# Spreading 128 node numbers over the partitions: two small DMAs through DRAM in place of a scaled identity and a product with ones

## The chip, the cores and the metric

The kernel runs on one core of a Trainium2 chip. Its metric is the device time of one execution in microseconds (us). Five engines work side by side, each through its own instructions in order, and they meet through semaphores: TensorE (PE: matmuls, with its weight loads shown apart as PEld), VectorE (DVE), ScalarE (ACT), GpSimd (POOL) and SyncE (SP), which here only issues DMAs. POOL issues DMAs too: the scatters that add rows of a tile to rows of a table in DRAM.

## What is computed

One layer of a graph network over 6,250 nodes with 128 features and 200,000 edges, sorted by `dst`:

```python
h = jnp.maximum(_layernorm(x, axis=-1), 0.0)
xw = h @ W_in                                            # a table of nodes
W_ij = shifted_softplus(f_ij @ W_f1 + b_f1) @ W_f2 + b_f2   # for each edge
W_ij = W_ij * f_ij_cutoff
x_ij = xw[dst] * W_ij
out = segment_sum(x_ij, src, num_segments=6250)
x = x + shifted_softplus(out @ W_o1 + b_o1) @ W_o2 + b_o2
```

`dst` is sorted, so the gather reads narrow windows of the table. `src` is random, so the sum over edges is the hard part.

## The kernel before

Edges are worked on in 391 groups of 512, called quads. A software pipeline written out by hand runs one iteration `i` for each quad and a few more at the end. In iteration `i` PE multiplies the gathered rows and the filter of quad `i-1` (L336, L339, L347), starts the filter of quad `i+1` (L289) and finishes quad `i-2`. ACT takes the soft plus of quad `i` (L294, L295, L300), DVE the product of quad `i-1` (L357). Further work hangs on named points of an iteration ("L", "D0", "D1", "A0", "DM", "PE2", "A2", "D2", "S", in that order of the text) through `at(iteration, point, function)`. The text's order is the order on each engine.

There are two kinds of quads.

- **Plain quads** (239). For each chunk of 128 edges PE multiplies an equality matrix with the messages, so that edges with the same node are summed in the chunk (L369). ACT copies the result to the tile `s` (L377, five buffers), DVE and ACT make the row numbers (L391, L398), and POOL issues four scatters that add the rows to an accumulator in DRAM (L417). That makes 955 scatters.
- **Permuted quads** (152: 8, 10, 13, 15, 18, 20 and so on, two and three apart in turn). A permutation on PE (L527) sorts the edges into 16 groups of nodes with 32 places each. Eight such quads are then summed at once by "units" (L605, L620, L631) into an accumulator in SBUF. Edges for which a group has no place left go to 64 overflow rows (L542 to L544), and ACT copies those to a tile `mo` (L550).

The overflow rows of two permuted quads make one tile of 128 rows, and a short chain takes each such pair to one more scatter (76 in all). For a pair whose second quad is `q`:

- `over_idx` (L558, DVE, iteration `q+5`): the node number of each row, a column `so` (shown as `ovs`) with one number for each partition.
- `over_dg` (L563 and L566, ACT, `q+6`): the 128x128 identity scaled by that column, and a small term `ojd` for the row number of the scatter.
- `over_row` (L571, PE, `q+6`): a matrix of ones times the scaled identity. Now each partition holds all 128 node numbers, in PSUM.
- `over_eq` (L576, DVE, `q+7`, point D0, the first of that iteration on DVE): which rows have the same node.
- `over_sum` (L581, PE, `q+8`), `over_copy` (L586, ACT), `over_ji` (L591, DVE), `over_int` (L595, ACT) and `over_scatter` (L417, POOL), all in `q+9`: rows of the same node are summed, and POOL scatters the sums.

Because quads lie two and three apart, `q` is a multiple of 5, and the pattern of hooks repeats every five iterations. `q+6` is even for one pair and odd for the next. `clear` moves a hook past iterations that hold a unit (they are multiples of 5 too).

SP issues, in every even iteration, the loads of two quads, `load_sc`: the features `ft` (L270), the node numbers `sb` (L272), the places `rb` (L275, two), four window numbers that are read into registers (L277), and four windows of the table `wn` (L282). Each waits for its buffer to come free. SP also issues the table's and features' loads and stores (L151, L233, L239, L259 to L261, L654). All of this is one queue in order.

PSUM has four banks with the tag "B" for the products `pp`, `pq`, `po`, `orow`, `osum` and `un`. The list `banked` names functions that take such a bank at the point PE2. An iteration with more than two of them is `full`, and then ACT copies `pp` within the same iteration, not early in the next.

The scatters go to four accumulators in turn (`acc_of`: three of them in the first 140 and in the last 64). A scatter waits for the landing of the one before it on the same accumulator. `scat` counts scatters by iteration, to place the early reading of accumulator 0. After the last scatter a tail reads the accumulators, sums them and applies the output layers (L1075 to L1138).

Of the kernel before, what the change touches and what calls it, by code (L numbers as in the profile page):

```python
# [7 lines left out]
F32 = mybir.dt.float32  # L8
# [5 lines left out]
ALU = mybir.AluOpType  # L14
# [6 lines left out]
P = 128  # L21
# [25 lines left out]
def tile_gnn(ctx: ExitStack, tc: tile.TileContext, x, fB, cT, srcT, srcr, dstr, win_, wf1, wf2, bias, bo1c, wo1,  # L47
             wo2, consts, ident, out, n_edges):
    nc = tc.nc
# [24 lines left out]
    mpi = {q: n for n, q in enumerate(mpq)}  # L74
    units = unit_its(mpq)
    plain = {q: n for n, q in enumerate(q for q in range(NQ) if q not in mpi)}
    scat = [0] * (NQ + 12)
# [1 line left out]
        if q not in mpi:  # L79
            scat[q + 4] += min(4, NCH - 4 * q)  # L80
    for q in mpq[1::2] + mpq[-1:] * (len(mpq) % 2):
        scat[q + 10] += 1
    RET = max(120, sum(scat) - 64)
    ret_at = min(i for i in range(len(scat)) if sum(scat[:i + 1]) >= RET)

    cp = ctx.enter_context(tc.tile_pool(name="cp", bufs=1))
    dp = ctx.enter_context(tc.tile_pool(name="dp", bufs=1, space=DRAM))
    edge = ctx.enter_context(ExitStack())
    ld = edge.enter_context(tc.tile_pool(name="ld", bufs=3))
    wk = edge.enter_context(tc.tile_pool(name="wk", bufs=2))  # L90
    sp_ = edge.enter_context(tc.tile_pool(name="sp", bufs=5))
    ps = edge.enter_context(tc.tile_pool(name="ps", bufs=2, space=PSUM))

    accs = []
    for k in range(NACC):
        a_ = dp.tile([ACC_R, P], F32, name=f"acc{k}")
        accs.append(a_)
    tab = dp.tile([NP * 3, P], BF16, name="tab")
    reld = dp.tile([NSC, SC], BF16, name="reld")
    src16 = dp.tile([NSC, SC], I16, name="src16")  # L100
# [7 lines left out]
    idt = cp.tile([P, P], F32, name="idt")  # L108
# [14 lines left out]
    iot = iotw[:, GN // 2:]  # L123
    tri = cp.tile([P, P], BF16, name="tri")
    onesb = cp.tile([P, P], BF16, name="onesb")
    onesf = cp.tile([P, P], F32, name="onesf")
    thr = cp.tile([P, GRP - 1], F32, name="thr")
    ge = cp.tile([P, 4 * RKQ, GRP + 1], BF16, name="ge")
    dropT = cp.tile([P, EP // P], BF16, name="dropT")
# [291 lines left out]
    mp = {}  # L421
# [136 lines left out]
        nc.vector.scalar_tensor_tensor(so, mo[:, P + 2:P + 3], float(GN), mo[:, P + 1:P + 2], op0=ALU.mult, op1=ALU.add)  # L558
        mp[q]["so"] = so

    def over_dg(q):
        dg = wk.tile([P, P], F32, tag="dg", name="dg", bufs=1)
        nc.scalar.mul(dg, idt, mp[q]["so"])  # L563
        mp[q]["dg"] = dg
        jd = sp_.tile([P, 2], F32, tag="ojd", name="ojd", bufs=3)
        nc.scalar.activation(jd[:, 0:1], mp[q]["so"], AF.Identity, bias=off)  # L566
        mp[q]["jd"] = jd

    def over_row(q):
        t = ps.tile([P, 512], F32, tag="B", name="orow", bufs=4)  # L570
        nc.tensor.matmul(t[:, :P], onesf, mp[q]["dg"], start=True, stop=True)  # L571
        mp[q]["row"] = t

    def over_eq(q):
        eq = wk.tile([P, P], F32, tag="oeq", name="oeq", bufs=1)
        nc.vector.tensor_scalar(eq, mp[q].pop("row")[:, :P], mp[q]["so"], None, op0=ALU.is_equal)  # L576
        mp[q]["eq"] = eq

    def over_sum(q):
# [90 lines left out]
    with tc.manual_schedule():  # L670
# [26 lines left out]
        onesc = cp.tile([P, 1], F32, name="onesc")  # L697
        nc.vector.memset(onesc, 1.0)
        nc.vector.memset(onesb, 1.0)
        nc.vector.memset(onesf, 1.0)  # L700
        nc.vector.memset(dropT, 0.0)
        nc.vector.memset(ge[:, :, 0:1], 1.0)
        nc.vector.memset(ge[:, :, GRP:], 0.0)
# [74 lines left out]
        def at(i, point, fn, *a):  # L778
            hooks.setdefault((i, point), []).append((fn, a))
# [121 lines left out]
        for r in range(-(-len(mpq) // RKQ)):  # L901
            i = mpq[RKQ * r]
            at(i - 5, "D2", rank_group, r)
            k = clear(i - 4, units)
            at(k, "PE2", rank_count, r)
            at(k + 1, "D0", rank_own, r)
            k = clear(k + 1, units)
            at(k, "PE2", rank_over, r)
            at(k + 1, "D0", rank_slot, r)
        for q in mpq:  # L910
            at(q + 1, "D2", perm_oh, q)
            at(q + 2, "D2", part_rem, q, 1)
            at(q + 2, "D2", part_rem, q, 2)
            for s in range(4):
                at(q + 3 + s // 2, "PE2", permute, q, s)
                at(q + 4 + s // 2, "A0", perm_out, q, s)
            at(q + 4, "PE2", over_pe, q)
            at(q + 5, "A0", over_out, q)
            if q == mpq[-1] and mpi[q] % 2 == 0:
                at(q + 4, "D2", over_none, q)  # L920
            if mpi[q] % 2 or q == mpq[-1]:
                at(q + 5, "DM", over_idx, q)
                at(q + 6, "A0", over_dg, q)
                k = clear(q + 6, units)
                at(k, "PE2", over_row, q)
                at(k + 1, "D0", over_eq, q)
                k = clear(q + 8, units)
                at(k, "PE2", over_sum, q)
                at(k + 1, "A0", over_copy, q)
                at(k + 1, "DM", over_ji, q)  # L930
                at(k + 1, "A2", over_int, q)
                at(k + 1, "S", over_scatter, q)
        last = mpq[-1]
        for r in range(len(mpq) // RND):
            for s, k in enumerate(unit_slots(mpq, r)):
                at(k - 1, "D2", unit_oh, r, s)
                at(k, "PE2", unit_pe, r, s)
                at(k + 1, "D1", unit_evac, r, s)

        banked = (prep_tp, prep_mm, rank_count, rank_over, permute, over_pe, over_row, over_sum, late_bias, r0_tp)  # L940
        full = {-1: False}
        r0_end = r0_at
        s1_pe(0)
# [63 lines left out]
    with tc.For_i(0, trips, 1) as ci:  # L1007
# [43 lines left out]
        eq = wk.tile([P, P], F32, tag="eq", name="feq")  # L1051
# [129 lines left out]
def unit_its(qs):  # L1181
    return {i for r in range(len(qs) // RND) for i in unit_slots(qs, r)}


def clear(i, busy, n=1):
    while any(i + k in busy for k in range(n)):
        i += 1
    return i
# [114 lines left out]
```

## Time and profile before

| | before |
|---|---|
| median of 3 runs | 2117.85 us (2117.82 to 2121.36) |
| the profiled execution | 2119.3 us |
| its span, first to last instruction | 2117.0 us |
| mean granted TensorE clock | 0.971 |
| PE / ACT / DVE / POOL busy, share of the span | 90% / 85% / 83% / 80% |
| scatters | 955 and 76, from 49.2 us to 2060.1 us |
| SP's longest wait | 510.3 us in 132 times, for DVE's L318 |

How to read the views. A row of the groups of instructions gives line, engine, operation, out<-in, shapes and count, then the busy time in us and the mean ns of one, then the time that the engine was idle just before them and what ended it. A row of the timeline gives start and length in us, engine, line, operation and count, with the idle time before it and what ended it in brackets. A row of the stretches gives each engine's busy time and number of instructions between two times. "issue" is idle time in which the engine waited for nothing that the profile shows.

### The profile page before, as it was taken

Reading aid. Unit: us, or ns where it says so; the run is one execution under the profiler, and the core shown is the slowest. Engines: PE = TensorE matmul, PEld = TensorE weight load, DVE = VectorE, ACT = ScalarE, POOL = GpSimd, SP = SyncE. Lnnn points to the kernel's source line nnn. Section 1 sums busy time; section 2 is a strip of 40 time slices with the busy share of each in tenths; the row PEclk is TensorE's granted clock in tenths of the full one; section 3 lists DMA queues with packets and bytes.
Section 4 is the critical chain, followed back from the end, with each engine's and each line's share of the span. In section 5 each row is a group of like instructions: output and inputs, shape, how many; then the busy total and the mean of one; then the engine's idle time right before and its main releaser. Section 6 shows DMA issues by size and latency. Waiting matters only on the chain.

```text
span 2117.0 us, 56533 instructions
## 1 busy us (share of the span) xinstructions
PE 1915.6 (90%) x19769; PEld 1392.3 (66%) x19769; DVE 1763.7 (83%) x4710; ACT 1789.3 (85%) x4781; POOL 1695.6 (80%) x1073
## 2 busy tenths in 40 slices
PE   3778999999999999998989999999999999998946
PEld 2556667676666667666767677777767666766724
DVE  4768888888989898888898989889888878897825
ACT  4688889998988899898989999999899898988804
POOL 2678888888888888888888888888888888887874
PEclk9899999999999999999999999999999999999977
DMA  7987767777777777777777777777777777777639
GB/s 265 242 183 132 149 129 146 141 157 144 149 141 147 133 151 145 141 145 142 148 133 157 139 136 152 143 146 152 136 146 139 129 152 137 139 154 144 111 38 241
DMA packets 395696, 315.17 MB, mean 149 GB/s; under 512 B 94959, under 2 KB 335130, under 8 KB 395410
## 3 DMA queue, kind: packets, MB, share of 16 engines
q1 hardware_dynamic: 245858, 240.57, 38.9%
q0 software_dynamic: 149264, 70.91, 35.3%
q8 instruction: 155, 2.54, 0.5%
q14 instruction: 131, 1.07, 0.2%
q10 hardware_dynamic: 288, 0.07, 0.0%
HBM read 173.32 MB, written 138.06 MB: 147 GB/s over the span
## 4 chain that ended last, share of the span: by engine, by line
PE 32%; ACT 20%; DVE 19%; DMA 10%; POOL 10%; issue 7%; SPq 2%; ACTq 0%; DVEq 0%; POOLq 0%
POOL acc L417 10%; DMA acc<-s,ji 8%; PE un L620 8%; PE W L347 7%; PE pq L527 6%; ACT xc L352 5%; PE pp L369 4%; ACT mst L533 3%; DVE so L605 3%; ACT e L295 3%; ACT e L294 2%; ACT e L300 2%; DVE pm L503 2%; ACT s L377 2%; DVE a L324 1%
## 5 line engine op out<-in xcount | busy, mean ns | idle before, releaser
L417 POOL DMA_INDIRECT acc<-s,ji x955 | 1538.3, 1611 | 350.3 <-issue 222.8
L527 PE MATMUL pq<-pt,pm 128*128 128x387 bf16 x2432 | 484.1, 339 | 26.5 <-ACT s L377 19.2
L352 ACT ACTIVATE xc<-xg,cb 128x128 f32<-128x128 f32 x1564 | 446.4, 374 | 46.9 <-PE xg L339 45.0
L347 PE MATMUL W<-w,a 128*128 128x128 f32 x3128 | 461.7, 292 | 0.0
L347 PEld LDWEIGHTS W<-w,a 128*128 128x128 f32 x3128 | 386.2, 194 | 41.8 <-issue 2.3
L620 PE MATMUL un<-so,mst 32*128 32x392 bf16 x7296 | 355.1, 331 | 41.8 <-DVE pr L467 18.4
L527 PEld LDWEIGHTS <-pm 128*128 128x128 bf16 x2432 | 238.6, 99 | 187.7 <-issue 36.1
L620 PEld LDWEIGHTS <-mst 32*128 32x128 bf16 x7296 | 223.0, 94 | 169.3 <-issue 63.0
L324 DVE SCALAR_TENSOR_TENSOR a<-z,e 128x512 f32<-128x512 f32 x391 | 267.2, 683 | 70.2 <-ACT e L300 70.0
L300 ACT ACTIVATE e<-e,con 128x512 f32<-128x512 f32 x391 | 282.3, 722 | 12.7
L369 PEld LDWEIGHTS pp<-m,eq 128*128 128x128 f32 x1912 | 255.0, 195 | 37.2 <-DVE accT L631 23.6
L369 PE MATMUL pp<-m,eq 128*128 128x129 f32 x1912 | 261.4, 280 | 17.0 <-DVE accT L631 15.0
L533 ACT CAST mst<-pq 128x387 bf16<-128x387 f32 x608 | 260.4, 480 | 8.3 <-PE pq L527 8.3
L377 ACT COPY s<-pp 128x258 f32<-128x258 f32 x478 | 167.1, 391 | 116.2 <-PE pp L369 64.8
L295 ACT ACTIVATE e<-e 128x512 f32<-128x512 f32 x391 | 246.5, 630 | 12.4
L294 ACT ACTIVATE e<-z 128x512 f32<-128x512 f32 x391 | 242.0, 619 | 16.7 <-PE z L289 16.1
L357 DVE TENSOR_TENSOR m<-W,xc 128x512 f32<-128x512 f32 x239 | 164.0, 686 | 80.4 <-ACT xc L352 75.4
L517 DVE TENSOR_TENSOR pt<-pt 128x512 f32<-128x512 f32 x304 | 209.9, 691 | 0.0
L503 DVE TENSOR_SCALAR pm<-iot,pos 128x576 bf16<-128x576 f16 x608 | 197.5, 387 | 0.0
L631 DVE TENSOR_TENSOR accT<-un,accT 128x392 f32<-128x392 f32 x288 | 142.5, 556 | 47.3 <-PE un L620 32.1
L357 DVE TENSOR_TENSOR pt<-W,xc 128x512 f32<-128x512 f32 x152 | 104.5, 688 | 82.1 <-ACT xc L352 80.7
L289 PE MATMUL z<-ft,ws 123*128 123x512 bf16 x391 | 151.9, 389 | 17.9 <-DMA ft<-fsd 17.9
(156 smaller groups left out, 2693.2 us busy)
## 6 DMA issues: line engine op xcount, KB each, us to landing
sb<-src SPq DMA_DIRECT2D x195, 256.0 KB
ft<-fsd SPq DMA_DIRECT2D x195, 240.0 KB
rb<-reld SPq DMA_DIRECT2D x391, 64.0 KB
fsd<-f SPq DMA_DIRECT2D x49, 480.0 KB
fb<-in_fB_dram SPq DMA_DIRECT2D x49, 320.0 KB
fsd<-f SPq DMA_DIRECT2D x49, 320.0 KB
acc<-s,ji POOLq DMA_INDIRECT x955
wn<-tab SPq DMA_DIRECT2D x782, 15.8 KB
```

What stands on the lines that cost most here:

```text
L294: nc.scalar.activation(e, st[q]["z"], AF.Abs)
L295: nc.scalar.activation(e, e, AF.Exp, scale=-1.0)
L300: nc.scalar.activation(e, e, AF.Ln, bias=half, scale=0.5)
L324: nc.vector.scalar_tensor_tensor(a, st[q]["z"], 0.0, st[q]["l"], op0=ALU.max, op1=ALU.add)
L347: nc.tensor.matmul(W[:, c, :], st[q]["a"][:, c * P:(c + 1) * P], w2, start=False, stop=(c == 3))
L352: nc.scalar.mul(xc[:, c, :], st[q]["xg"][:, c, :], late["c", q // CQ][:, 4 * (q % CQ) + c:4 * (q % CQ) + c + 1])
L357: nc.vector.tensor_tensor(m[:, :, :P], st[q]["W"], st[q]["xc"], op=ALU.mult)
L369: nc.tensor.matmul(pp[:, c, :129], st[q]["eq"][:, k, :], m[:, k, :129], start=True, stop=True)
L417: nc.gpsimd.indirect_dma_start(out=accs[k][:, :], out_offset=bass.IndirectOffsetOnAxis(ap=ji, axis=0), in_=s, in_offset=None, compute_op=A ...
L527: nc.tensor.matmul(t[:, :PW], mp[q]["pm"][:, c, s * P:(s + 1) * P], high(mp[q]["pt"][:, c:c + 1, :PW])[:, 0], start=(c == 0), stop=(c == 3))
L533: nc.scalar.copy(mp[q]["ms", s][:, :PW], mp[q].pop(("q", s))[:, :PW])
L620: nc.tensor.matmul(ts[g][:, :GN], mp[q]["ms", s][v, k * P:(k + 1) * P], mp[q]["oh"][v], start=(q == qs[0] and k == 0), stop=(q == qs[-1] a ...
```

## The change

The 128 node numbers are written from SBUF to a row of a small table `ordr` in DRAM, one number from each partition, and read back as that row repeated on all partitions. The first DMA is issued in `q+6`, the second in `q+7`, both by SP and at the end of the iteration's text. `over_eq` moves from `q+7` to `q+9` and reads SBUF, `over_sum` from `q+8` to `q+9`, and what follows it from `q+9` to `q+10`. The scaled identity and the product with ones go, and so does the PSUM bank that the product took.

```diff
-        scat[q + 10] += 1
+        scat[q + 11] += 1
...
+    ordr = dp.tile([2, P], F32, name="ordr")
...
-    onesf = cp.tile([P, P], F32, name="onesf")
...
-    def over_dg(q):
-        dg = wk.tile([P, P], F32, tag="dg", name="dg", bufs=1)
-        nc.scalar.mul(dg, idt, mp[q]["so"])
-        mp[q]["dg"] = dg
+    def over_put(q):
+        nc.sync.dma_start(ordr[mpi[q] // 2 % 2].rearrange("(p o) -> p o", o=1), mp[q]["so"])
+
+    def over_get(q):
+        row = wk.tile([P, P], F32, tag="dg", name="orow", bufs=1)
+        nc.sync.dma_start(row, ordr[mpi[q] // 2 % 2:mpi[q] // 2 % 2 + 1, :].to_broadcast([P, P]))
+        mp[q]["row"] = row
+
+    def over_jd(q):
         jd = sp_.tile([P, 2], F32, tag="ojd", name="ojd", bufs=3)
         nc.scalar.activation(jd[:, 0:1], mp[q]["so"], AF.Identity, bias=off)
         mp[q]["jd"] = jd

-    def over_row(q):
-        t = ps.tile([P, 512], F32, tag="B", name="orow", bufs=4)
-        nc.tensor.matmul(t[:, :P], onesf, mp[q]["dg"], start=True, stop=True)
-        mp[q]["row"] = t
-
     def over_eq(q):
         eq = wk.tile([P, P], F32, tag="oeq", name="oeq", bufs=1)
-        nc.vector.tensor_scalar(eq, mp[q].pop("row")[:, :P], mp[q]["so"], None, op0=ALU.is_equal)
+        nc.vector.tensor_scalar(eq, mp[q].pop("row"), mp[q]["so"], None, op0=ALU.is_equal)
...
-        nc.vector.memset(onesf, 1.0)
...
                 at(q + 5, "DM", over_idx, q)
-                at(q + 6, "A0", over_dg, q)
-                k = clear(q + 6, units)
-                at(k, "PE2", over_row, q)
-                at(k + 1, "D0", over_eq, q)
-                k = clear(q + 8, units)
+                at(q + 6, "A0", over_jd, q)
+                at(q + 6, "S", over_put, q)
+                at(q + 7, "S", over_get, q)
+                at(q + 9, "D0", over_eq, q)
+                k = clear(q + 9, units)
                 at(k, "PE2", over_sum, q)
...
-        banked = (prep_tp, prep_mm, rank_count, rank_over, permute, over_pe, over_row, over_sum, late_bias, r0_tp)
+        banked = (prep_tp, prep_mm, rank_count, rank_over, permute, over_pe, over_sum, late_bias, r0_tp)
```

## The prediction

> **What bounds the kernel now.** I read the page's busy shares first. PE is busiest, which suggests PE, but a share is a mean over stages. So I went to the groups of instructions, and there to the engine that has one kind of work from start to end, POOL. First the two groups of scatters, then stretches of the span (columns: PE, PEld, DVE, ACT, POOL busy with counts, PE clock, DMA share, GB/s):
>
> ```profile
> PE 1915.6 (90%) x19769; PEld 1392.3 (66%) x19769; DVE 1763.7 (83%) x4710; ACT 1789.3 (85%) x4781; POOL 1695.6 (80%) x1073
> L417 POOL DMA_INDIRECT acc<-s,ji x955 | 1538.3, 1611 | 350.3 <-issue 222.8
> L417 POOL DMA_INDIRECT acc<-os,oji x76 | 121.7, 1601 | 24.5 <-issue 7.6 <-ACT mst L533 4.0 <-ACT xc L352 3.1
> ```
>
> ```profile
> 100.00:300.00 200.00, 173.37 (x1588) 126.59 (x1586) 157.11 (x425) 170.21 (x463) 159.26 (x100) 0.94 0.77 152
> 550.00:1110.00 560.00, 524.82 (x5590) 380.53 (x5589) 498.30 (x1387) 500.17 (x1353) 470.26 (x292) 1.00 0.75 143
> 1110.00:1550.00 440.00, 429.58 (x4606) 314.12 (x4605) 390.96 (x1021) 407.90 (x1096) 369.97 (x230) 1.00 0.76 146
> ```
>
> POOL is shown 80% busy, but between two scatters there is a gap of 0.30 or 0.31 us that belongs to the scatter (the timeline rows below). From 550 to 1110 us, 292 scatters x 0.30 = 87.6, and 470.3 + 87.6 = 557.9 of 560. From 1110 to 1550 it is 370.0 + 69.0 = 439.0 of 440. POOL has no free time there. From 49.2 us (first scatter) to 2058.6 (last), 1,030 steps take 2009.4 us: 1.951 each, against 1.54 + 0.31 = 1.85 for an undisturbed one.
>
> Next, how far POOL lags: from the end of a pair's row numbers (`oji`) to its scatter.
>
> ```profile
> 1116.80 0.37 ACT L595 ACTIVATE oji<-ojd,con 128x1 int32<-128x1 f32 x1
> 1120.67 1.62 POOL L417 DMA_INDIRECT acc<-os,oji  x1 [0.31 <-ACT ji L398]
> ```
> ```profile
> 2037.01 0.29 ACT L595 ACTIVATE oji<-ojd,con 128x1 int32<-128x1 f32 x1 [2.89 <-DVE ojd L591]
> 2058.57 1.54 POOL L417 DMA_INDIRECT acc<-os,oji  x1 [0.31 <-issue]
> ```
>
> The reader is to see a queue of finished work in front of POOL: 21.3 us long at the end. Pairing all 76 `oji` with their scatters in order, it is 22.2 us for the first pair (162 us), 20.4 at 419, 14.3 at 620, 12.3 at 997, 3.5 at 1121 (the row above, the shortest), 10.6 at 1321, 21.3 at 1595, and about 21 from there. So PE, ACT and DVE are some 3% slower than POOL from 550 to 1110 and live on the reserve; elsewhere they are faster and are held back by the five `s` buffers. POOL sets the time from about 100 us to 2060, and a tail of 57 us that the change doesn't touch follows.
>
> **The change, part by part.** "Iteration" is about 5 us (1966 us over 390 steps of L324).
>
> ```profile
> L571 PE MATMUL orow<-dg,onesf 128*128 128x128 f32 x152 | 32.9, 299 | 7.5 <-ACT s L377 4.6 <-DVE accT L631 1.9
> L563 ACT ACTIVATE dg<-idt,ovs 128x128 f32<-128x128 f32 x76 | 29.5, 389 | 5.4 <-DVE ovs L558 5.2
> L576 DVE TENSOR_SCALAR oeq<-orow,ovs 128x128 f32<-128x128 f32 x76 | 26.0, 342 | 1.1 <-PE orow L571 1.1
> L581 PE MATMUL osum<-mo,oeq 128*128 128x132 f32 x152 | 29.8, 277 | 0.5 <-DVE accT L631 0.5
> ```
>
> - *Removed:* 32.9 us of PE (0.43 a pair), 29.5 us of ACT (0.39), and a memset at the start, off the path. POOL is worth nothing of this: 0 of 1,031 scatters go. I take 0 us. With POOL out of the way PE would give at most its 32.9 + 7.5 = 40.4.
> - *Reserve:* 560 us hold some 22 pairs, so PE gets back up to 22 x 0.43 = 9.5 us just where the queue runs down. That lengthens the shortest queue and still gives no time.
> - *The two DMAs, issue:* 152 more on SP at about 0.36 us each (the L654 issues: 362 ns), 55 us in all. SP waits 510.3 us for DVE's L318 alone (132 times) before its next loads, so this is covered. In the pairs with `q+6` even the read waits for the write's landing, with the next `load_sc` behind it. That holds SP about 3 us (stores of features, L261, land 1.4 to 5.3 us after issue, median 2.8, by the semaphore records). Those loads are wanted three iterations later, some 15 us: 0 us. What is late if it isn't covered: `ft`, then L289 on PE.
> - *The two DMAs, landing:* no row has this one. Below it: the last scatter, 128 rows of 512 B as here, 3.22 us in the chain of waits with 1.54 of POOL in it, so 1.7. Above it: tail loads of 256 KB, 4.9 to 5.8 us. Nearest is L654's load (128 rows of 256 B): its semaphore rises 1.55 us after the issue's end in the median of 25, 2.8 in the slowest tenth. I take 1.55.
> - *Is `over_eq` late?* It is the first on DVE in `q+9`, and behind it in order stand L308 and L324, then PE's L347. With `q+6` even the read is issued right after the write; from the end of SP's last `wn` in `q+6` to DVE's D0 of `q+9` are 6.0 to 13.6 us (median 10.1), and 0.47 + 2.8 + 0.47 + 1.55 = 5.3 are needed (0.47: 0.07 to the next issue and 0.40 for it): never late. With `q+6` odd the read stands behind the whole `load_sc` of `q+7`, which waits for DVE. From SP's last DMA there to D0 are -0.4 to 4.9 us, median 2.4, and 0.47 + 1.55 = 2.0 are needed. Laid against the 37 odd pairs of this trace one by one, 13 are late by 15.5 us in all (4 of them with 4.6 us between 550 and 1110). With 2.8 for the landing it is 40.8 us (11.7 there), with 4.0 it is 85.2 (26.4). Outside that stretch the queue of about 20 us covers it. Inside it 4.6 stands against 9.5 of PE and a reserve of 3.5: 0 us.
> - *`over_eq` and `over_sum` in one iteration:* before, a whole iteration lay between them. In iterations `q+9` PE ends L369 1.85 us (median) after the new `over_eq` could end; of 74, 5 are late, by 1.8 us in all. 0.
> - *PSUM banks:* `q+9` now asks for six of four (pp, pp, osum, pq, pq, po), before five, and `q+6` for four, before five. The fifth waits for ACT's copy of the first `pp`; PE has 0.52 + 0.39 + 0.78 us of work until then, and a copy takes 0.39. 0, or 0.3 us a pair if ACT is behind, less than the PE time freed.
> - *`over_eq` reads SBUF, not PSUM:* does it stretch POOL's scatter? The nearest row is L184, the same kind of instruction from SBUF:
>
> ```profile
> 999.05 1.54 POOL L417 DMA_INDIRECT acc<-s,ji  x1 [0.30 <-ACT e L295]
> 999.51 0.69 DVE L184 TENSOR_SCALAR xn<-x_sb,mv,rs 128x128 f32<-128x128 f32 x2
> 1006.44 1.71 POOL L417 DMA_INDIRECT acc<-s,ji  x1 [0.30 <-issue]
> ```
>
> The scatter that covers both L184 took 1.54 us, the undisturbed length. Other neighbours make 1.71. So 0 to 76 x 0.17 = 13 us, and I take 0, by the nearest row.
>
> The Trainium skill speaks against that: "SBUF — State Buffer", section "Who interferes with whom", says that a tensor_scalar from SBUF may enter a two-port mode on DVE, and then DVE and GpSimd shut each other out for a whole instruction. By that rule the sum would be up to 76 x 0.34 = 26 us longer; the L184 row shows no such block, and no run here shows the new instruction yet.
>
> Sum: each of these terms is 0 on POOL's path, so no change. The profiled execution has a span of 2117.0 and a time of 2119.3, so 2.3 lie around it; the median of the runs is 2117.85, 1.5 below. I predict 2118. One per cent is 21 us; 0.2%, about what a measurement of this kernel can tell from no change (its three runs differ by 0.17%), is 4.2 us.
>
> **The rivals.**
> - *Slower: the read lands late and DVE waits in order.* It decides from the point where lateness between 550 and 1110 us passes the reserve of 3.5 us; only there does POOL run dry, and what it loses is not made up. With a landing of 2.8 us and nothing back from PE: 11.7 - 3.5 = 8, 2126. With 4.0: 26.4 - 3.5 = 23, 2141. With the full credit of 9.5 the latter is 13, 2131. For it: a margin of 2.4 us against a need of 2.0. Against it: 25 similar loads with 1.55.
> - *Faster: POOL's steps shorten.* Idle before scatters is 350.3 + 24.5 = 374.8 us, of which 1031 x 0.30 = 309.3 is their own gap and 24 the wait for the first. The rest, 41.5, is mostly waits for an accumulator's landing, some 15 us of them before 100 us, which the change doesn't touch. If freed engines took away a quarter: 2107.
> - *PE is the bound after all*, as its 90% says: minus 32.9 to 40.4, 2078 to 2085. Against it stands the queue of 21 us at the end.
> - *The stretched scatter:* up to +13, 2131; it goes with the slower side.
>
> **How the numbers follow.** No change 0.50 (2114 to 2122). Slower 0.31: late read 0.24, stretch 0.07. Faster 0.19: shorter steps 0.15, PE 0.04. Both signs hold half of the chance, more than my sum alone would leave them, since every zero above rests on a cover that was measured in the old order of work. The time is that of the likeliest, 2118. The range leaves out PE's case and the worst of the late read: 2107 to 2138; the likeliest's own is 2114 to 2122.
>
> **What would show it.** Right: POOL's busy time plus 0.30 a scatter still fills 550 to 1110 and 1110 to 1550; the queue at the end is still about 21 us; the shortest queue is longer than 3.5 us, or at least not gone; ACT's L377 waits longer for `acc`. The late read would show as DVE waiting for `orow`, at L576, tens of times, and POOL waiting for ACT's `ji` near 1100 us. The stretch would show as a mean of L417 above 1611 ns. It is wrong if the last scatter ends more than 4 us from 2060.

## The result, and the profile after

After the change the kernel takes 2430.41 us (median of six runs, 2416.45 to 2436.67), before 2117.23 (six runs, 2113.17 to 2121.36): the ratio is 1.147, with a 95% interval of 1.1437 to 1.1508. The prediction of no change (2118, 2107 to 2138) was wrong, by an amount that none of its cases reached. The profiled execution took 2425.07 us, with a span of 2423.0 and a mean granted clock of 0.912.

The span grew by 306.0 us. The last scatter ends at 2365.7 us instead of 2060.1, which is 305.6 later, and the tail after it is 57.3 instead of 56.9. So all but 0.4 us of it was lost while POOL scatters. First the busy shares and the groups of instructions of after:

```profile
PE 1994.4 (82%) x19617; PEld 1406.6 (58%) x19617; DVE 1763.5 (73%) x4709; ACT 1775.8 (73%) x4705; POOL 1695.8 (70%) x1073
L417 POOL DMA_INDIRECT acc<-s,ji x955 | 1536.2, 1609 | 656.4 <-DMA acc<-s,ji 288.6
L377 ACT COPY s<-pp 128x258 f32<-128x258 f32 x478 | 158.5, 377 | 300.6 <-DMA acc<-s,ji 228.3
L576 DVE TENSOR_SCALAR oeq<-orow,ovs 128x128 f32<-128x128 f32 x76 | 25.4, 334 | 291.2 <-DMA orow<-ordr 291.2
```

POOL's busy time is what it was (1695.8 against 1695.6), and so is the length of a scatter (1609 ns against 1611). What grew is the idle time before the scatters, from 350.3 to 656.4 us, by 306.1, and it has another name now: not "issue", which is the scatter's own gap, but `DMA acc<-s,ji`, the landing of the scatter before it on the same accumulator. L377 names the same landings, because its five `s` buffers come free only then. The third group is the forecast's own rival, DVE waiting for the row that is read back: 291.2 us of idle time, as long as what POOL waits for landings. Which of the two is the cause can't be read from these rows.

The stretches of after, with the columns of those shown of before (PE, PEld, DVE, ACT, POOL busy with counts, PE clock, DMA share, GB/s):

```profile
550.00:1110.00 560.00, 490.73 (x4961) 345.17 (x4960) 438.29 (x1212) 439.88 (x1185) 408.87 (x253) 0.93 0.84 129
1110.00:1550.00 440.00, 387.14 (x3948) 272.38 (x3949) 346.00 (x934) 352.45 (x939) 328.14 (x204) 0.94 0.83 130
```

From 550 to 1110 POOL's 253 scatters and their gaps fill 408.9 + 253 x 0.30 = 484.8 of 560 us. Before, it was 557.9. Every engine is less busy, and the DMA rings are busier while they move less (0.84 and 129 GB/s against 0.75 and 143). POOL does not starve: paired with their scatters as in the prediction, the 76 `oji` are ready 19.6 us ahead or more, where the shortest queue of before was 3.5. Work lies in front of POOL all the time, and POOL waits for something else.

The waits of after (who waited at which line, for what: us in total, times, longest):

```profile
DVE oeq L576 <- DMA orow<-ordr: 291.2, 72, 8.2
POOL acc L417 <- DMA acc<-s,ji: 291.0, 140, 8.3
...
ACT s L377 <- DMA acc<-s,ji: 228.3, 78, 9.6
...
PE osum L581 <- DVE oeq L576: 67.8, 33, 4.8
```

Before, POOL's row was:

```profile
POOL acc L417 <- DMA acc<-s,ji: 50.9, 81, 5.4
```

Now a single write, the one issued at 1050.23 us. First SP's and POOL's timeline of after, then its stretches of 1 us:

```profile
1050.23 0.35 SPq L562 DMA_DIRECT2D ordr<-ovs  x1
...
1060.66 0.36 SPq L566 DMA_DIRECT2D orow<-ordr  x1
```
```profile
1054.07 1.54 POOL L417 DMA_INDIRECT acc<-s,ji  x1 [0.30 <-issue]
1055.91 2.00 POOL L417 DMA_INDIRECT acc<-s,ji  x1 [0.30 <-issue]
1060.15 1.54 POOL L417 DMA_INDIRECT acc<-s,ji  x1 [2.24 <-DMA acc<-s,ji]
```
```profile
1052.00:1053.00 1.00, 1.00 (x11) 0.81 (x11) 1.00 (x5) 1.00 (x3) 0.78 (x1) 1.00 0.90 143
...
1054.00:1055.00 1.00, 1.00 (x9) 0.61 (x8) 0.76 (x2) 1.00 (x4) 0.93 (x1) 1.00 1.38 33
1055.00:1056.00 1.00, 1.00 (x11) 0.58 (x10) 0.96 (x4) 0.94 (x3) 0.70 (x2) 1.00 0.30 27
1056.00:1057.00 1.00, 1.00 (x15) 0.80 (x13) 1.00 (x3) 1.00 (x3) 1.00 (x1) 1.00 0.44 63
...
1058.00:1059.00 1.00, 0.98 (x9) 0.81 (x8) 0.76 (x2) 0.00 (x0) 0.00 (x0) 1.00 0.94 171
```

The last two columns tell it (the share counts the whole time of a packet in the stretch in which it starts, so it can pass 1). Between 1052 and 1056 us what all rings move falls from 143 to 27 GB/s, while the engines still work on what they have; at 1058 ACT and POOL stand still as well. The read, which stands behind the next loads on SP, goes out 10.4 us after the write. Counted over all 76 writes, the packets of more than 16 B that start in each us after the write's issue fall from 117 in the second us to 45 to 61 in the fourth to ninth, and are back at 155 in the eleventh. With the same write spread out, each number 512 B from the next (an experiment below), they are 131 to 153 in the fourth to ninth.

Landings, from the end of the issue to the rise of the semaphore, in us. Part of the semaphore records is missing: at least 14 of the 16 records of a landing are there for 922 of the 955 scatters before, but for 382 after, and for 193 and 77 of the 196 loads of `ft`. So the columns of after are rough; with the write alone (the first experiment), where 904 scatters have them, the slowest tenth begins at 8.31.

| | before: median, slowest tenth from | after: median, slowest tenth from |
|---|---|---|
| scatter L417 | 2.50, 3.86 | 3.23, 9.38 |
| load of `ft`, L270 | 3.45, 4.56 | 4.41, 10.31 |
| write of `ordr`, L562 | | 8.51, 9.54 |
| read of `ordr`, L566 | | 3.82, 5.57 |

Other loads and scatters, which have nothing to do with `ordr`, became as slow as the write. Why that stops POOL follows from the rows of before: the scatters go to four accumulators in turn, a step is 1.85 us, so an accumulator is due again 4 x 1.85 - 1.54 = 5.86 us after its scatter's issue ends. A landing of 3.9 hides in that, one of 9.4 does not. The trace of before bears the sum out: for the first 140 scatters and the last 64, with at most three accumulators in turn, the same sum gives no more than 4.01 us, and of the 37.0 us that POOL is idle beyond its gap after the first scatter, 33.2 lie before these and 3.8 before the 827 others. POOL's idle time beyond its gap within 14 us after a write is 305 us in the 76 pairs, 4.0 each; in all after the first 100 us it is 328.6, before 21.8.

### The profile page after: what moved, and what is told of

Same layout as the page of the kernel before. It is cut to its first block, busy times and chain, and to the rows that moved or that the text cites. A ratio compares the mean times of both kernels' runs of the same rounds, so it can differ in the third digit from the quotient of the medians.

```text
span 2423.0 us, 56398 instructions
## 1 busy us (share of the span) xinstructions
PE 1994.4 (82%) x19617; PEld 1406.6 (58%) x19617; DVE 1763.5 (73%) x4709; ACT 1775.8 (73%) x4705; POOL 1695.8 (70%) x1073
## 5 line engine op out<-in xcount | busy, mean ns | idle before, releaser
L417 POOL DMA_INDIRECT acc<-s,ji x955 | 1536.2, 1609 | 656.4 <-DMA acc<-s,ji 288.6
L527 PE MATMUL pq<-pt,pm 128*128 128x387 bf16 x2432 | 533.1, 362 | 129.8 <-ACT s L377 97.4
L347 PE MATMUL W<-w,a 128*128 128x128 f32 x3128 | 475.8, 297 | 0.0
L527 PEld LDWEIGHTS <-pm 128*128 128x128 bf16 x2432 | 250.8, 104 | 318.0 <-issue 182.5
L347 PEld LDWEIGHTS W<-w,a 128*128 128x128 f32 x3128 | 399.6, 200 | 44.6 <-issue 8.2
L377 ACT COPY s<-pp 128x258 f32<-128x258 f32 x478 | 158.5, 377 | 300.6 <-DMA acc<-s,ji 228.3
L620 PE MATMUL un<-so,mst 32*128 32x392 bf16 x7296 | 326.7, 329 | 13.4 <-ACT s L377 5.6
L369 PE MATMUL pp<-m,eq 128*128 128x129 f32 x1912 | 270.2, 286 | 55.5 <-ACT s L377 41.4
L620 PEld LDWEIGHTS <-mst 32*128 32x128 bf16 x7296 | 196.9, 94 | 132.3 <-issue 28.2
L576 DVE TENSOR_SCALAR oeq<-orow,ovs 128x128 f32<-128x128 f32 x76 | 25.4, 334 | 291.2 <-DMA orow<-ordr 291.2
L339 PE MATMUL xg<-wn,oh 63*128 63x128 bf16 x1564 | 163.5, 228 | 7.5 <-DMA wn<-tab 2.7
```

The source lines that it names most:

```text
L347: nc.tensor.matmul(W[:, c, :], st[q]["a"][:, c * P:(c + 1) * P], w2, start=False, stop=(c == 3))
L369: nc.tensor.matmul(pp[:, c, :129], st[q]["eq"][:, k, :], m[:, k, :129], start=True, stop=True)
L417: nc.gpsimd.indirect_dma_start(out=accs[k][:, :], out_offset=bass.IndirectOffsetOnAxis(ap=ji, axis=0), in_=s, in_offset=None, compute_op=A ...
L527: nc.tensor.matmul(t[:, :PW], mp[q]["pm"][:, c, s * P:(s + 1) * P], high(mp[q]["pt"][:, c:c + 1, :PW])[:, 0], start=(c == 0), stop=(c == 3))
L620: nc.tensor.matmul(ts[g][:, :GN], mp[q]["ms", s][v, k * P:(k + 1) * P], mp[q]["oh"][v], start=(q == qs[0] and k == 0), stop=(q == qs[-1] a ...
```

## The experiments

Twelve kernels were run. Times are medians, and ratios are to the kernel before on the same chip in the same session, with a 95% interval. Theory A: the write holds the DMA rings. Theory B: DVE waits in order for the row read back. Theory C: it is the read.

**The write alone, the read alone, the rest without the write, and all of it with a later comparison.** The first two leave the kernel before as it is, with its identity and its product, and add one DMA whose data nobody uses:

```diff
...
+    def over_put(q):
+        nc.sync.dma_start(ordr[mpi[q] // 2 % 2].rearrange("(p o) -> p o", o=1), mp[q]["so"])
...
+                at(q + 6, "S", over_put, q)
```

> The kernel before, with the write of 128 numbers to DRAM added in q+6 and nobody reading it; the scaled identity and the product stay. Theory A (the 128 four-byte writes into one 512 B row hold the DMA rings for about 7 us, and scatters and loads land late): the write lands 7 to 9 us after its issue as in the changed kernel, POOL waits some 250 us for landings on an accumulator, and the time is 2300 to 2430 us. Theory B (what costs is DVE, which waits 291 us in order for the row read back): nobody waits here, so 2113 to 2122 us. In between: both.

```diff
...
+    def over_get(q):
+        row = wk.tile([P, P], F32, tag="xrow", name="xrow", bufs=1)
+        nc.sync.dma_start(row, ordr[mpi[q] // 2 % 2:mpi[q] // 2 % 2 + 1, :].to_broadcast([P, P]))
...
+                at(q + 7, "S", over_get, q)
```

> The kernel before, with only the read added: a row of DRAM that is written once at the start is read onto all 128 partitions in q+7, and nobody uses it. Theory A and B: 2113 to 2122 us, no change, and the read lands about 2 us after its issue. Theory C (the 128 reads of one 512 B row are what holds the rings): 2200 us or more.

The third is after without the write. The row holds 1e9 everywhere, and the comparison is "greater or equal": all 128 overflow rows are summed into one, here and in the two later kernels that compare with a constant.

```diff
-        nc.vector.tensor_scalar(eq, mp[q].pop("row"), mp[q]["so"], None, op0=ALU.is_equal)
+        nc.vector.tensor_scalar(eq, mp[q].pop("row"), mp[q]["so"], None, op0=ALU.is_ge)
...
-                at(q + 6, "S", over_put, q)
```

> The changed kernel without the write: the row read back is a constant, and the comparison is made 'greater or equal', so that all 128 overflow rows are summed into one (that part of the sum is not the reference's; every instruction but the write is there). Theory A: 2113 to 2122 us, as before the change, since POOL's 1031 scatters set the pace and the 0.43 us of PE and 0.39 us of ACT freed for each pair are worth nothing; DVE hardly waits at L576. Theory B with the wait caused by the order of SP's queue alone: 2300 or more. If PE was the bound after all: 2078 to 2085.

The fourth is after with the comparison and all behind it three iterations later, so that the row is there when DVE comes to it.

```diff
-                at(q + 9, "D0", over_eq, q)
-                k = clear(q + 9, units)
+                at(q + 12, "D0", over_eq, q)
+                k = clear(q + 12, units)
```

> The changed kernel with the comparison and all that follows three iterations later (q+12, q+13), so that the row has 15 us more to land. Theory A: DVE's wait at L576 is gone, but POOL still waits some 250 us for landings: 2300 to 2420 us. Theory B: 2113 to 2130 us.

| | time | ratio | the write lands, median | POOL waits for landings on `acc` |
|---|---|---|---|---|
| before, same session | 2110.8 | | | |
| write alone | 2386.4 | 1.1315 [1.1293, 1.1338] | 7.95 | 300.4 |
| read alone | 2116.41 | 1.0031 [1.0018, 1.0044] | | 47.3 |
| no write | 2131.01 | 1.0096 [1.0075, 1.0117] | | 47.3 |
| all, later comparison | 2380.82 | 1.1289 [1.1266, 1.1312] | 7.81 | 250.3 |

The write alone, read by nobody, costs 275.6 of the 313.2 us. Its chain of waits and its group of scatters (in this kernel L418):

```profile
DMA 37%; POOL 22%; ACT 14%; issue 10%; PE 10%; DVE 5%; SPq 2%; ACTq 0%; DVEq 0%; POOLq 0%
...
L418 POOL DMA_INDIRECT acc<-s,ji x955 | 1526.3, 1598 | 598.5 <-DMA acc<-s,ji 274.8
```

The chain that ended last runs through landings for 37% of the span. In before it was 10%:

```profile
PE 32%; ACT 20%; DVE 19%; DMA 10%; POOL 10%; issue 7%; SPq 2%; ACTq 0%; DVEq 0%; POOLq 0%
```

Nothing but the write was added, so theory A holds for the main part and C falls: the read alone costs 0.3%. Theory B holds for a small part. With the later comparison DVE's wait at L576, 291.2 us, is gone, but the time falls only by the difference of the ratios, 0.018 or about 39 us, and ends where the write alone stood. Most of that long wait lay beside POOL's own.

**What about the write is dear?** Theory A1: the 128 numbers lie side by side in one piece of 512 B of DRAM and queue up there. Theory A2: any write of 4-byte pieces does it. All of these are the write alone, as above, with another pitch or fewer numbers:

```diff
-    ordr = dp.tile([2, P], F32, name="ordr")
+    ordr = dp.tile([2, P, P], F32, name="ordr")
...
+        nc.sync.dma_start(ordr[mpi[q] // 2 % 2][:, 0:1], mp[q]["so"])
```

> The kernel before with the write alone, as in the run of the write alone, but each of the 128 numbers goes to a row of 512 B of its own. Theory A1 (the writes queue up because all 128 go into one 512 B row): the write lands about 2 us after its issue, POOL's waits for an accumulator fall back to about 50 us, 2107 to 2122 us. Theory A2 (any write of 4 bytes to DRAM is that slow, wherever it goes): about 2386 us, as with one row.

With `[2, P, 16]`, a pitch of 64 B:

> The same write alone, each number 64 B from the next: 8 numbers in each stretch of 512 B, 16 such stretches. A1 with 512 B as the unit: groups of 8 queue up, landing some 1 us later than with rows of their own, 2107 to 2150 us. A1 with 64 B or less as the unit: as with rows of their own. A2: about 2386 us.

With the packed row again, but 32 numbers only:

```diff
+        nc.sync.dma_start(ordr[mpi[q] // 2 % 2].rearrange("(p o) -> p o", o=1)[:32], mp[q]["so"][:32])
```

> The same write alone into one 512 B row, but of 32 numbers, not 128. A1: the time in the queue goes with the count: 8.0 us less 2 for 128, so about 3.5 us to the landing for 32, and the time is between 2115 and 2190 us (a quarter of 275 us is 69, less where the first microseconds are covered). If it were a fixed cost of such a write: about 2386 us.

With `[2, P, 8]`, a pitch of 32 B, and with `[2, P, 4]`, 16 B:

> The write alone, each number 32 B from the next, as in the runs with 64 B and 512 B. If numbers queue up only within the same 32 B or less: landing 2 us, 2107 to 2122 us. If within the same 64 B: pairs queue up, landing some 0.1 us later at most if that alone counts, and 2107 to 2135 us. If the cost is instead one of a 512 B stretch hit by many: more than 2150.

> The same at 16 B from the next: four numbers to 64 B, two to 32 B. As with 64 B if only the same 16 B or less collide: landing 2 us, 2107 to 2122 us; if the unit is 64 B: a landing between 2.2 and 4 us and 2120 to 2220 us. The kernel with 128 numbers in one 512 B row (32 times 16 B, 8 times 64 B) took 2386 us.

| numbers, pitch | time | ratio | lands, median (us) | latest scatter landing around each write, mean | POOL waits for landings on `acc` |
|---|---|---|---|---|---|
| 128, 4 B | 2386.4 | 1.1315 [1.1293, 1.1338] | 7.95 | 9.03 | 300.4 |
| 32, 4 B | 2219.49 | 1.0495 [1.0437, 1.0552] | 4.96 | 6.78 | 164.5 |
| 128, 16 B | 2125.7 | 1.0035 [1.0019, 1.0051] | 2.60 | | 59.2 |
| 128, 32 B | 2120.22 | 1.0000 [0.9986, 1.0015] | 2.18 | | 49.2 |
| 128, 64 B | 2113.8 | 0.9996 [0.9975, 1.0018] | 2.17 | | 42.8 |
| 128, 512 B | 2113.73 | 0.9996 [0.9973, 1.0018] | 2.09 | 3.62 | 47.5 |

The same 128 four-byte pieces, the same instruction and the same queue: at 32 B apart they cost nothing, side by side they cost 13%. A2 falls. At 16 B, where two numbers share 32 B, there is a small cost, 0.35% with a landing of 2.60; at 32 B, where two share 64 B, there is none. With 32 packed numbers both the landing (3.5 expected) and the time (2115 to 2190) passed what was expected, so the landing does not simply go with the number of pieces: the first 32 add 2.87 us to the 2.09 of the spread write, the next 96 another 2.99. The group of scatters at a pitch of 512 B and with 32 packed numbers:

```profile
L418 POOL DMA_INDIRECT acc<-s,ji x955 | 1527.2, 1599 | 355.7 <-issue 219.9
```
```profile
L418 POOL DMA_INDIRECT acc<-s,ji x955 | 1530.9, 1603 | 451.0 <-issue 207.9
```

At 512 B the idle time is that of before (350.3); with 32 packed numbers it is about 100 more, and the time is 103.8 us longer. The fifth column of the table lies beside the 5.86 us at which an accumulator is due: what goes over it is 3.2 us a pair for 128 numbers (mean over the pairs that the records give; time lost 275.6 / 76 = 3.6), 1.0 for 32 (lost 1.4) and none at 512 B (lost none). As far as these three rows go, that is the price of a held ring, and it starts only where the landing that it delays is longer than the slack.

**What the removed work was worth.** The kernel before without the scaled identity and the product; the comparison takes a constant tile, 1e9 everywhere, instead of the row.

```diff
-        nc.scalar.mul(dg, idt, mp[q]["so"])
...
-        nc.tensor.matmul(t[:, :P], onesf, mp[q]["dg"], start=True, stop=True)
...
-        nc.vector.tensor_scalar(eq, mp[q].pop("row")[:, :P], mp[q]["so"], None, op0=ALU.is_equal)
+        nc.vector.tensor_scalar(eq, onesf, mp[q]["so"], None, op0=ALU.is_ge)
```

> The kernel before with the scaled identity (L563) and the product with ones (L571) left out and nothing in their place: the comparison reads a constant tile in SBUF, 'greater or equal', so that all 128 overflow rows are summed into one (that part of the sum is not the reference's). The order of the rest stays. POOL as the bound: 2107 to 2116 us, no gain from 32.9 us of PE and 29.5 us of ACT. PE as the bound: about 2078 us. It also tells which part of the 20 us of the changed kernel without its write comes from the read and the later comparison.

2125.79 us, ratio 1.0047 [1.0031, 1.0063]: with 33 us of PE and 30 us of ACT gone it is no faster, a little slower if anything, and above the 2107 to 2116 us that were expected. The freed time went into the queue in front of POOL: its shortest length rose from 3.5 to 10.8 us, at the same place, near 1125 us. One execution's 3.5 is not to be leaned on: in five kernels that keep this work and add only a harmless DMA (the read alone, and the writes at 16 to 512 B) it is 0.3 there, while without the write it is 11.0. ACT waited longer for landings at L377, 67.5 us against 31.1. In its trace the last scatter ends 5.2 us later than in that of before, and the scatters add up to 5.1 us more (1615 ns on average against 1610); POOL's idle time is the same, 374.8. Why the scatters are longer is open.

**The rest, some 1%.** Without the write the time was 2131.01 us, above the 2113 to 2122 that were expected. Is the rest the late read (theory L) or something else (R)? The kernel without the write once more, with its comparison three iterations later:

> The changed kernel without its write (constant row, 'greater or equal', one sum of all 128 rows, as in the run without the write), and with the comparison and what follows three iterations later. The run without the write was 0.96% slower than before, with DVE waiting 65 us at the comparison. Theory L (that rest is the read landing late): DVE's wait goes, and the time is between 0.3 and 0.5% above before, as with the read alone or with the removal alone. Theory R (the rest is POOL's own steps, 1620 ns a scatter against 1610, and a changed order of work): still 0.7 to 1.2% above.

2136.03 us, ratio 1.0082 [1.0059, 1.0106], against 1.0096 with the comparison in its place. DVE's wait at the comparison, 65.4 us in 36 times there, is gone, and the time stays, as R said. But this kernel alone does not settle it, since the later comparison has a price of its own: from 550 to 1110 us POOL is idle beyond its gap for 14.5 us (1.1 with the comparison in its place), and the last scatter waits 4.2 us for its row numbers, while the scatters add up to 13.6 us less in this trace. The kernel with the comparison in its place settles it better: 1.1 us from 550 to 1110 is what before has there (1.0), and the shortest queue is 11.0 us, so the late read did not let POOL run dry. Its last scatter ends 16.8 us later than in before: 10.5 us are longer scatters (1620 ns on average), and 6.5 are idle time, most of it near the start and the end. By size the rest could be the read (0.31%) and what the kernel with the constant comparison lost (0.47%), but that these two are its parts was not tried, and why the scatters are longer is open.

**The whole change with the write mended.** Each number is written four times over, so that the pieces are 16 B and lie 16 B apart, and the read brings 2 KB to each partition.

```diff
...
-        so = sp_.tile([P, 1], F32, tag="ovs", name="ovs", bufs=3)
+        so = sp_.tile([P, 4], F32, tag="ovs", name="ovs", bufs=3)
...
-        nc.sync.dma_start(ordr[mpi[q] // 2 % 2].rearrange("(p o) -> p o", o=1), mp[q]["so"])
+        nc.sync.dma_start(ordr[mpi[q] // 2 % 2].rearrange("(p o) -> p o", o=4), mp[q]["so4"])
...
-        row = wk.tile([P, P], F32, tag="dg", name="orow", bufs=1)
+        row = wk.tile([P, 4 * P], F32, tag="dg", name="orow", bufs=1)
...
-        mp[q]["row"] = row
+        mp[q]["row"] = row[:, ::4]
```

> The complete change, with every node number written four times over: each partition writes 16 B, so 128 pieces lie 16 B apart in a row of 2 KB; the read brings 2 KB to each partition (256 KB in all, four times as much as in after), and the comparison takes every fourth number of it. Theory A1 (the loss comes from 128 four-byte pieces that lie side by side in one piece of 512 B): what was measured one by one adds up, the write alone at 16 B +7 us, read and later comparison without a write about +20 us, so 2120 to 2155 us (at most 1.02 times before), the write landing in 2 to 3 us (median) and POOL waiting for landings on its accumulator 45 to 75 us. Theory A2 (any write of small pieces that is read back at once, or a path through DRAM as such, holds the rings): 2350 us or more, the write landing in 6 us or more. In between, near 2200, if the read of 256 KB to all partitions holds the scatters in the write's place: then the read lands in more than 5 us and POOL's wait is above 100 us. Not below before in any theory, since POOL sets the time and no scatter goes.

2159.81 us (2149.04 to 2160.34, four runs), ratio 1.0150 [1.0102, 1.0197]. The write lands in 2.30 us, the read in 4.17 (medians). Its waits:

```profile
POOL acc L417 <- issue: 231.1, 746, 3.0
DVE oeq L576 <- DMA orow<-ordr: 116.4, 51, 6.6
...
POOL acc L417 <- DMA acc<-s,ji: 65.7, 90, 5.2
```

POOL's wait for landings is back from 291.0 to 65.7. The same data by the same route, in pieces of 16 B, takes back 13 of the 15% of the change, and what is left is somewhat above the 2120 to 2155 us that were expected. Of the 40.1 us by which its last scatter is later than in before, 29 are idle time, 15 of them in the row of landings above, and 11 are longer scatters (1621 ns on average). No run of the twelve was faster than the kernel before by more than its interval.

## Why the prediction was wrong

- **The step that failed** is "The two DMAs, issue", with the landing it took for the write: "stores of features, L261, land 1.4 to 5.3 us after issue, median 2.8". The write landed in 8.5, outside the range of that row. But a larger number in that place would not have been enough: the prediction asked only who waits for the write (SP, the read, DVE), never what the write does to transfers that have nothing to do with it. That term was missing from the sum, and it is 275.6 of the 313.2 us. The sum held the landings of the scatters fixed, or let them shrink. L261 stores rows of features, not single numbers. No row of before had the property that counted, many 4-byte pieces in one place, and the prediction neither said so nor bounded it.
- **Where it could have been seen as a risk:** POOL waits for the landing of the scatter before it on the same accumulator, due 5.86 us after the issue, against 3.86 for the slowest tenth and 6.29 at worst in before. The prediction counted this wait among the gains ("if freed engines took away a quarter") and did not ask what happens if landings grow.
- **"That holds SP about 3 us":** 203.6 us in 29 times, 7.0 each. The row of SP's waits in after:

```profile
SPq L272 <- DVE eq L318: 237.9, 71, 7.8
SPq L566 <- DMA ordr<-ovs: 203.6, 29, 9.7
```

  The cover held all the same. SP's wait for L318 shrank from 510.3 to 237.9, and PE's wait for `ft` at L289 is 17.2 us (before 17.9).
- **The read's landing,** taken as 1.55 between bounds of 1.7 and 4.9 to 5.8 from other rows: 3.05 to 3.09 where no write was in its way. L654's load was not near enough; the middle of the bounds was.
- **"Is `over_eq` late?"** "Never" in the pairs with an even `q+6`, 13 of 37 odd pairs by 15.5 us: in after 72 of 76 pairs were late, by 291.2 us. Without the write 36 were, by 65.4 us, near the 85 of the rival with a landing of 4.0. The rival's price was to come from POOL running dry from 550 to 1110 us, and there POOL lost nothing (1.1 us idle beyond its gap, 1.0 in before). Only together with the slow write did it cost something, about 39 us. So the rival "the read lands late" was a real mechanism, but not the one that decided.
- **Right:** POOL sets the time (its busy time is unchanged, and all 305.6 us came before its last scatter); removed work of PE and ACT is worth no time and goes into the queue (credit worked out as up to 9.5 us; in the kernel without the identity and the product it is 10.8 - 3.5 = 7.3, and 10.5 against the kernels that had 0.3); the tail does not change (57.3 against 56.9).
- **The comparison from SBUF** does not stretch the scatters in after: past 100 us the 74 that lie over one take 1547 ns on average, the other 938 take 1613. With the later comparison it is 1650 for 70 of them against 1607, which would be 3 us in all, so where it falls may matter a little. The Trainium skill's page "SBUF — State Buffer", section "Who interferes with whom", would have allowed a block of a whole instruction, some 340 ns here. No run shows such a block: in after the longest of the 74 takes 1802 ns, 260 more than the median of all scatters.
- **`over_sum` in the same iteration and the PSUM banks** cannot be priced from after: PE waits 67.8 us at L581 for the late comparison, and that hides what they cost.

## What to carry to other kernels

A transfer has two prices: the wait for its own landing, and what it does to the landings of all others. Before a small DMA is added, find the wait of the bounding engine that depends on a landing and work out its slack (here 5.86 us against 3.86 of landing); what held a landing longer than that was paid nearly in full here, at each write. Where each partition writes one number to DRAM, give every number a place of its own 32 B away from the next, or keep it on the chip: here the product with ones cost nothing, since the engines that did it had time.

## What the runs showed of the hardware

- 128 four-byte pieces written side by side into 512 B land in 7.95 us and keep other transfers back for some 6 to 7 us; at 16 B apart it is 2.60 us, at 32 B 2.18, at 512 B 2.09. Between 32 and 128 packed numbers the landing grows by 2.99 us, 31 ns for each further number on average.
- The records of the write's own packets do not show this: the 4-byte packets of its queue that start within 2.5 us of a write of after take 178 ns at most, their median over the run is 9. The packets of others are long: one of 2048 B normally takes 84 ns, and 8.8 us at worst.
- What goes on below the packets is not settled. The Trainium skill's page "DMA: Bandwidth & Descriptors", section "Specifications", says that below 512 B the DMA engine reads, modifies and writes. Size alone does not decide here: four-byte pieces 32 B apart cost nothing. "Collectives: The Full Stack", section "Rules for kernel authors", asks for buffers aligned to 32 B against the same thing; the rows at 16 and 32 B fit that, though it is said of other transfers. But 32 packed numbers share their pieces of 32 B just as 128 do and lose 104 us, not 276, so pieces of 32 B that queue each for itself do not explain it. No run shows the reading and modifying itself.
- The mean granted clock was lower in the runs with long stalls: 0.912 in after, 0.933 with the write alone, 0.962 with 32 numbers, 0.971 before. PE was not what POOL waited for, and the cause of this was not looked into.
